# A graph layer on one core: where in a step VectorE makes its first one-hots, and which engine reads the placed sums first

## The chip, the core and the metric

The kernel runs on one core of a Trainium2 chip. The core has five engines with instruction queues of their own: TensorE (PE: matmuls, with PEld for its weight loads), VectorE (DVE), ScalarE (ACT), GpSimd (POOL) and SyncE (SP, which here only starts transfers). They meet through semaphores. The metric is the time of one execution on the device in microseconds (us); lower is better. Before the change the median of three runs is 1567.36 us (1563.31 to 1572.13).

## The reference

A message-passing layer over a graph of 6250 nodes with 64 features and 200000 edges, sorted by destination, with a residual and a layer norm around it:

```
w    = silu(edge_attr @ W1 + b1) @ W2 + b2                # 32 -> 64 -> 9 per edge
msg  = einsum('ef,em,fmg->eg', x[src], edge_sh * w, W_tp) # 64 x 9 x 64
agg  = segment_sum(msg, dst) / sqrt(16)
gamma, beta = split(silu(c_noise[:,None] @ Wn1 + bn1) @ Wn2 + bn2)
out  = layernorm(x + agg * (1 + gamma) + beta)
```

Everything is float32.

## The kernel before

**Tiling.** The edges are cut into tiles of 128, and 16 tiles make a block; there are 98 blocks and 49 groups of 128 nodes. The main loop runs over i = 0 to 97. Its order is written out by hand: what a step calls first stands first in each engine's queue. In one step different blocks are at different stages.

**Rows of the sources.** The tile `hs` of a block holds the 64 features of each edge's source. Most of its 16 tiles are fetched by indirect DMAs, one per tile, which GpSimd issues for block i+6 at the head of step i (`gather`, line 91). The last 3 or 4 tiles of a block (`picked`) are not fetched: `pick` (lines 463 to 486) selects them with matmuls. VectorE makes a one-hot `hot_k` (`hots`, line 460, 128 x 896) from the edge's key, which ScalarE has spread into PSUM (`keys`, line 454, bank tag "r"). TensorE multiplies it with the table `xs`, split in two parts, in 14 matmuls into `px` (line 475, two banks), and VectorE selects and sums the result into `hs` (lines 484 and 486). In every sixth block one more tile is fetched row by row by SyncE (line 106).

**Weights and messages.** For block i+2, `hidden` computes the first layer (line 403, bank tag "p1") and ScalarE the silu (`st`, line 411). For block i+1, `second` (line 420, bank tag "s") computes the second layer, and `weights` turns it and builds `a`, which holds the nine weights times a one-hot of the destination (lines 430, 436, 442). `windows(i)` multiplies `hs` with `a` (line 504), ScalarE copies the result into `zt` (line 514), and in odd steps `project` applies W_tp to two blocks (line 543, the bank of tag "p1" again) and turns the result (line 549); `halves` splits it in two parts `r` and makes one-hots `c` of the nodes (lines 524 to 528).

**Nodes.** `nodes(i)` takes the one bank of tag "s", called `ps`, and returns small parts that `pick` runs one by one behind its matmul pairs:
- `product`, the gate's matmul for node group i-2 (line 589), as long as i-2 is below 49;
- in even steps `place`: two matmuls (line 559) add the projected rows into the node columns `pd`. VectorE adds the carry of the pair before to the left half (`yt`, line 565), and ScalarE copies the right half as the new `carry` (line 568);
- in every fourth step (i = 7, 11, ..., 95) `bring`: two matmuls (line 576) turn two node groups back, and `finish_nodes` (lines 669 to 683) does gate, residual and layer norm on VectorE, with the square root on ScalarE. I call these finish steps;
- `gate`: VectorE reads the product into `gam` and `xb` (lines 355 and 356), in steps 2 to 50.

After these reads the "s" bank is free, and `second(i+1)` takes it for line 420 in the same step.

**Order in a step.** gathers and loads; `keys(i+2)` and the first two one-hots of block i+2; `pick(i+1, 0)` with the parts of `nodes(i)` inside it; the other one-hots; `hidden(i+2)`; `second(i+1)`; `windows(i)`; `project`; `pick(i+1, 1)` with the parts of `weights` and the turning inside it; the remaining picks.

Of the kernel before, what the change touches and what calls it, by code (L numbers as in the profile page):

```python
# [7 lines left out]
F32 = mybir.dt.float32  # L8
# [7 lines left out]
P = 128  # L16
N, F, M, D, H, E = 6250, 64, 9, 32, 64, 200000
NJ = 49
# [26 lines left out]
def pair(q):  # L45

    return [g for g in (2 * q - 1, 2 * q) if 0 <= g < NBLK]


def picked(g):  # L50

    return Q - (3 * g % 8 < 3)


def tiles(g):
    return min(KB, NT - g * KB)
# [3 lines left out]
def gnn_resnorm_kernel(ctx: ExitStack, tc: tile.TileContext, x, src, dst, dst_row, ea, sh, cn,  # L60
                       w1, b1, w2, b2, wtp, wn1, bn1, wn2, bn2, out):
    nc = tc.nc
# [16 lines left out]
    with ExitStack() as fast:  # L79
        loads = fast.enter_context(tc.tile_pool(name="loads", bufs=3))  # L80
        work = fast.enter_context(tc.tile_pool(name="work", bufs=2))
# [16 lines left out]
        def load_rows(g, e0):  # L98
            for e in range(e0, min(e0 + SPR, P), 8):
                n = min(8, min(e0 + SPR, P) - e)  # L100
                _, vs = nc.values_load_multi_w_load_instructions(
                    src_r[SPG.index(g):SPG.index(g) + 1, e:e + n], engines=[mybir.EngineType.SP],
                    min_val=0, max_val=NPAD - 1,
                    skip_runtime_bounds_check_because="src is below N, as for the gathers")
                for k in range(n):
                    nc.sync.dma_start(hs[g][e + k:e + k + 1, 0, :], x[bass.ds(vs[k], 1), :])
# [246 lines left out]
        def gate(j, pe):  # L353

            nc.vector.tensor_scalar(gam[:, j, :], pe[:, 0:F], 1.0, 0.25, op0=ALU.add, op1=ALU.mult)
            nc.vector.tensor_add(xb[:, j, :], xb[:, j, :], pe[:, F:2 * F])  # L356
# [94 lines left out]
        def keys(g):  # L451

            pk_t[g] = psum.tile([P, Q, P], F32, tag="r", name=f"pk{g}")
            nc.scalar.copy(pk_t[g][:, 0:picked(g), :], kr_t.pop(g))  # L454

        def hots(g, t0, t1):

            for t in range(t0, min(t1, picked(g))):
                hot_k[g, t] = late.tile([P, J, P], F32R, tag="hot_k", name=f"hot_k{g}_{t}", bufs=7)
                nc.vector.tensor_tensor(hot_k[g, t], pk_t[g][:, t, None, :].to_broadcast([P, J, P]),  # L460
                                        nk.unsqueeze(2).to_broadcast([P, J, P]), op=ALU.is_equal)

        def pick(g, t, other=()):


            other = [f for fs in other for f in fs]
            q = picked(g) if g < NBLK else 0
            if t >= q:
                for f in other:
                    f()  # L470
                return
            px = psum.tile([P, F, J], F32, tag="px", name=f"px{g}_{t}", bufs=2)
            for h in range(J):
                for i in range(2):
                    nc.tensor.matmul(px.rearrange("p f l -> p (f l)"), hot_k[g, t][:, h, :],  # L475
                                     xs[i][:, h].rearrange("p f l -> p (f l)"),
                                     start=(h == 0 and i == 0), stop=(h == J - 1 and i == 1))
                    if i == 1 and other:
                        other.pop(0)()
            for f in other:  # L480
                f()
            xm = late.tile([P, F, J], F32, tag="xm", name=f"xm{g}_{t}")
            c = (g + 1) * Q - q + t
            nc.vector.scalar_tensor_tensor(xm, li[:, None, :].to_broadcast([P, F, J]), jl[:, c:c + 1], px,  # L484
                                           op0=ALU.is_equal, op1=ALU.mult)
            nc.vector.tensor_reduce(hs[g][:, tiles(g) - q + t, :], xm, AX.X, ALU.add)  # L486
# [31 lines left out]
        r, hot, carry, yt = {}, {}, {}, {}  # L518
# [35 lines left out]
        def place(q, pd):  # L554

            gs = pair(q)

            def part(k):
                nc.tensor.matmul(pd, r[q][:, k].rearrange("p s f -> p (s f)"), hot.pop(gs[k]),
                                 start=(k == 0), stop=(k == len(gs) - 1))  # L560
                if k == len(gs) - 1:
                    r.pop(q)
                    if q > 0:
                        yt[q - 1] = work.tile([P, P], F32, tag="yt", name=f"yt{q}", bufs=3)
                        nc.vector.tensor_add(yt[q - 1], pd[:, 0:P], carry.pop(q - 1))  # L565
                    if q < NJ:
                        carry[q] = work.tile([P, P], F32, tag="carry", name=f"carry{q}")
                        nc.scalar.copy(carry[q], pd[:, P:2 * P])  # L568

            return [lambda k=k: part(k) for k in range(len(gs))]  # L570

        def bring(j0, j1, py):


            def part(j):
                nc.tensor.matmul(py[:, j - j0], yt.pop(j), ident2, start=True, stop=True)
                if j == j1 - 1:
                    finish(j0, j1, py[:, 0:j1 - j0])

            return [lambda j=j: part(j) for j in range(j0, j1)]  # L580

        def nodes(i):


            ps = psum.tile([P, 4, P], F32, tag="s", name=f"ps{i}")
            parts = []
            if 0 <= i - 2 < NJ:
                def product(j=i - 2):
                    nc.tensor.matmul(ps[:, 2], ht[j // 4 % 2][:, j % 4], wn2a, start=True, stop=True)
                parts.append(product)  # L590
            if i % 2 == 0 and i >= 2:
                parts += place(i // 2 - 1, ps[:, 0:2].rearrange("p a n -> p (a n)"))
            j = (i - 5) // 2
            if i % 2 == 1 and i >= 5 and j % FB == FB - 1:
                parts += bring(j + 1 - FB, j + 1, ps[:, 3].rearrange("p (j f) -> p j f", f=F))
            if 0 <= i - 2 < NJ:
                parts.append(lambda: gate(i - 2, ps[:, 2]))
            return parts

        with tc.manual_schedule(), tc.tile_pool(name="temp", bufs=1) as temp:  # L600
            setup(temp)

            for i in range(NBLK):
                if i + AHEAD < NBLK:
                    gather(i + AHEAD)
                if i % LB == 0 and i + LB < NBLK:
                    if i > 0:
                        load(i + LB)
                    near(i + LB)
                if i % LB == 1 and i + 1 + LB < NBLK:  # L610
                    load_keys(i + 1 + LB)
                if i % 4 == 3 and i + 1 < NJ:
                    gate_load(i + 1)
                for g in SPG:
                    if 0 < g - i <= AHEAD:
                        load_rows(g, (AHEAD - g + i) * SPR)
                if i + 2 < NBLK:
                    keys(i + 2)
                    hots(i + 2, 0, 2)
                pick(i + 1, 0, [nodes(i)])  # L620
                if i + 2 < NBLK:
                    hots(i + 2, 2, Q)
                if 3 <= i <= 5:
                    reach(i - 3)
                if i + 2 < NBLK:
                    hidden(i + 2)
                if i + 1 < NBLK:
                    second(i + 1)
                if i < NBLK - 2:
                    windows(i)  # L630
                turn = project(i // 2) if i % 2 == 1 else []
                if i % 4 == 1 and i - 1 < NJ:
                    gate_hidden(i - 1)
                if i + 1 < NBLK:
                    pick(i + 1, 1, [weights(i + 1), turn])
                for t in range(2, Q):
                    pick(i + 1, t)
                if i == NBLK - 1:
                    for f in turn:
                        f()  # L640
                    ps = psum.tile([P, 4, P], F32, tag="s", name="ps_l")
                    for f in place(i // 2, ps[:, 0:2].rearrange("p a n -> p (a n)")):
                        f()
                    py = psum.tile([P, FB, F], F32, tag="r", name="py_l")
                    for f in bring(NJ - 3, NJ - 1, py):
                        f()
                if i >= NBLK - 2:
                    windows(i)
                if i == NBLK - 2:
                    sums(i + 1)  # L650
            project(NBLK // 2)
            ps = psum.tile([P, 4, P], F32, tag="s", name="ps_n")
            for f in place(NBLK // 2, ps[:, 0:2].rearrange("p a n -> p (a n)")):
                f()
            for f in bring(NJ - 1, NJ, psum.tile([P, 1, F], F32, tag="r", name="py_n")):
                f()
# [201 lines left out]
```

## Time and profile before

The profiled execution took 1570.09 us; its span from first to last instruction is 1568.3 us. The granted TensorE clock was 0.972 of full speed on average.

| engine | busy us | share | instructions |
|---|---|---|---|
| PE | 1460.5 | 93% | 10810 |
| PEld | 1208.6 | 77% | 10810 |
| DVE | 1139.5 | 73% | 1987 |
| ACT | 528.6 | 34% | 1335 |
| POOL | 1129.5 | 72% | 1201 |

| group | count | mean ns | busy us |
|---|---|---|---|
| L475 px matmuls | 4970 | 375 | 1100.8 |
| L91 gathers | 1192 | 946 | 1128.2 |
| L460 hot_k | 355 | 1081 | 370.5 |
| L484 xm | 355 | 677 | 240.4 |
| L486 sum into hs | 355 | 620 | 220.1 |
| L442 a | 98 | 1353 | 132.6 |
| L411 st | 98 | 1114 | 109.2 |
| L568 carry | 48 | 265 | 12.7 |

Matmuls overlap and their ends are modelled, so a busy PE row is not PE at its peak. In a row of the groups, the first number after the bar is the busy time, the second the mean of one, and behind the second bar stands the engine's idle time just before such instructions with what ended it. In a row of waits the numbers are the total, the count and the longest. A timeline row has start, length, engine, line, operation, result <- operands, how many are merged, and in brackets the idle time before it with what ended it.

### The profile page before, as it was taken

To read this page: it belongs to the slowest core of one execution; us is meant where nothing else is said; L and a number is where in the kernel's file an instruction comes from. 1 tells how busy PE (TensorE), PEld (TensorE's weight loads), DVE (VectorE), ACT (ScalarE), POOL (GpSimd) and SP (SyncE) were. 2 spreads that over 40 slices of the span, in tenths; PEclk is the share of its full clock that TensorE was granted. 3 is DMA by queue.
4 is the path that set the end of the run, shared out by engine and by line. 5 is a ranking of instruction groups with operands and counts; after the bars stand their busy time and mean duration, and the time that the engine had idled before them with its cause. 6 is when DMAs were issued, how large, how long until landed. Compare 5 with 4: busy or idle time off the path is not lost.

```text
span 1568.3 us, 34363 instructions
## 1 busy us (share of the span) xinstructions
PE 1460.5 (93%) x10810; PEld 1208.6 (77%) x10810; DVE 1139.5 (73%) x1987; ACT 528.6 (34%) x1335; POOL 1129.5 (72%) x1201
## 2 busy tenths in 40 slices
PE   4998999999999999999999999999999999999995
PEld 2787778778787788787877877877877878778774
DVE  5686777777777777777777777777777677777773
ACT  4232242433332423332333323323233332333331
POOL 7777777777777777777777777777777777777700
PEclk9999999999999999999999999999999999999997
DMA  5321222222222222222222222222222222222200
GB/s 166 93 62 55 53 75 51 63 56 71 57 62 65 63 54 61 56 71 59 58 71 53 59 53 71 59 53 70 53 60 55 68 54 58 71 53 59 71 7 5
DMA packets 90939, 96.16 MB, mean 61 GB/s; under 512 B 37161, under 2 KB 51451, under 8 KB 90748
## 3 DMA queue, kind: packets, MB, share of 16 engines
q1 hardware_dynamic: 51842, 53.09, 11.5%
q0 software_dynamic: 38144, 39.14, 11.4%
q8 instruction: 88, 1.44, 0.4%
q10 hardware_dynamic: 762, 1.64, 0.3%
q14 instruction: 103, 0.84, 0.2%
HBM read 92.04 MB, written 1.73 MB: 60 GB/s over the span
## 4 chain that ended last, share of the span: by engine, by line
PE 51%; POOL 20%; DVE 13%; issue 8%; DMA 4%; ACT 3%; SPq 0%; DVEq 0%; POOLq 0%; ACTq 0%
PE px L475 37%; POOL hs L91 20%; DVE hot_k L460 5%; PE pz L504 5%; DMA hs<-in_x_dram,src_i 4%; PE pt L543 3%; PE p L420 2%; DVE xm L484 2%; DVE hs L486 2%; PE p L403 1%; PE p L430 1%; ACT L411 1%; ACT st L411 1%; DVE oh L382 1%; ACT carry L568 1%
## 5 line engine op out<-in xcount | busy, mean ns | idle before, releaser
L91 POOL DMA_INDIRECT hs<-in_x_dram,src_i x1192 | 1128.2, 946 | 364.0 <-issue 335.0
L475 PE MATMUL px<-xs,hot_k 128*128 128x448 f32 x4970 | 1100.8, 375 | 8.4 <-DVE xs L294 7.8
L475 PEld LDWEIGHTS px<-xs,hot_k 128*128 128x128 f32 x4970 | 903.3, 190 | 96.7 <-issue 12.2
L484 DVE SCALAR_TENSOR_TENSOR xm<-li,jl,px 128x448 f32<-128x448 f32 x355 | 240.4, 677 | 220.2 <-PE px L475 217.9
L460 DVE TENSOR_TENSOR hot_k<-pk,nk 128x896 fp32r<-128x896 f32 x355 | 370.5, 1081 | 2.3 <-ACT pk L454 2.3
L486 DVE TENSOR_REDUCE hs<-xm 128x64 f32<-128x448 f32 x355 | 220.1, 620 | 12.5 <-DVE xm L484 0.2
L514 ACT COPY zt<-pz 64x160 f32<-64x160 f32 (+2 forms) x784 | 213.3, 272 | 23.0 <-PE pz L504 13.9
L411 ACT ACTIVATE st<-p,b1c 128x1024 f32<-128x1024 f32 x98 | 109.2, 1114 | 296.1 <-PE p L403 295.8
L568 ACT COPY carry<-ps 128x128 f32<-128x128 f32 x48 | 12.7, 265 | 390.2 <-DVE yt L565 382.4
L436 DVE TENSOR_TENSOR p<-p,sh 128x72 f32<-128x72 f32 x196 | 47.3, 241 | 132.7 <-ACT rt L546 47.7
L504 PEld LDWEIGHTS pz<-a,hs 128*64 128x64 f32 x3126 | 110.6, 142 | 41.9 <-issue 38.4
L442 DVE TENSOR_TENSOR a<-oh,p 128x1152 f32<-128x1152 f32 x98 | 132.6, 1353 | 3.3
L504 PE MATMUL pz<-a,hs 128*64 128x72 f32 x3126 | 125.5, 236 | 1.1 <-DMA hs<-in_x_dram,src_i 0.6
L403 PE MATMUL p<-ea,w1bd 64*128 64x512 f32 x392 | 113.5, 656 | 0.0
L420 PEld LDWEIGHTS p<-st,w2p 128*32 128x32 f32 x784 | 16.6, 108 | 113.3 <-issue 52.7
L543 PE MATMUL pt<-zt,wtc 128*64 128x128 f32 x960 | 72.8, 305 | 27.7 <-ACT st L411 26.0
L420 PE MATMUL p<-st,w2p 128*32 128x256 f32 x784 | 63.7, 395 | 35.7 <-DVE xb L356 32.0
L543 PEld LDWEIGHTS pt<-zt,wtc 128*64 128x64 f32 x960 | 62.2, 157 | 29.7 <-ACT st L411 27.8
L679 ACT ACTIVATE var<-var,eps 128x2 f32<-128x2 f32 (+1 forms) x25 | 7.4, 296 | 220.5 <-DVE var L678 220.5
L430 PE MATMUL p<-ident,p2s 128*128 128x128 f32 x196 | 54.4, 278 | 0.0
L454 ACT CAST pk<-kr 128x384 f32<-128x384 f16 (+1 forms) x98 | 53.9, 550 | 1.5 <-DMA kr<-kd 1.4
L403 PEld LDWEIGHTS p<-ea,w1bd 64*128 64x128 f32 x392 | 30.2, 188 | 28.8 <-issue 27.9
(122 smaller groups left out, 530.0 us busy)
## 6 DMA issues: line engine op xcount, KB each, us to landing
hs<-in_x_dram SPq DMA_DIRECT2D x2048, 0.2 KB
ea<-in_ea_dram SPq DMA_DIRECT2D x49, 512.0 KB
hs<-in_x_dram,src_i POOLq DMA_INDIRECT x1192
kr<-kd SPq DMA_DIRECT2D x49, 256.0 KB
sh<-in_sh_dram SPq DMA_DIRECT2D x49, 144.0 KB
cb<-cn_d SPq DMA_DIRECT2D x12, 128.0 KB
out_dram<-o SPq DMA_DIRECT2D x24, 64.0 KB
gam<-in_x_dram ACTq DMA_DIRECT2D x2, 448.0 KB
```

Source lines behind the costliest of these rows:

```text
L91: hs_dma[g] = [nc.gpsimd.indirect_dma_start(out=hs[g][:, t - g * KB, :], out_offset=None, in_=x, in_offset=bass.IndirectOffsetOnAxis(ap=sr ...
L403: nc.tensor.matmul(p1[:, i, :], w1bd[i * 64:(i + 1) * 64, :], e[i * 64:(i + 1) * 64, :], start=True, stop=True)
L411: nc.scalar.activation(st[g], p1_t.pop(g), AF.Silu, bias=b1c)
L420: nc.tensor.matmul(p2[g][c * D:(c + 1) * D, 0, :].rearrange("p (i e) -> p i e", i=2), w2p, s[:, :, c * P:(c + 1) * P], start=True, stop=True)
L442: nc.vector.tensor_mul(a[g], oh_t.pop(g)[:, :, None, :].to_broadcast([P, KB, M, W]), sw.unsqueeze(3).to_broadcast([P, KB, M, W]))
L460: nc.vector.tensor_tensor(hot_k[g, t], pk_t[g][:, t, None, :].to_broadcast([P, J, P]), nk.unsqueeze(2).to_broadcast([P, J, P]), op=ALU.is_ ...
L475: nc.tensor.matmul(px.rearrange("p f l -> p (f l)"), hot_k[g, t][:, h, :], xs[i][:, h].rearrange("p f l -> p (f l)"), start=(h == 0 and i ...
L484: nc.vector.scalar_tensor_tensor(xm, li[:, None, :].to_broadcast([P, F, J]), jl[:, c:c + 1], px, op0=ALU.is_equal, op1=ALU.mult)
L486: nc.vector.tensor_reduce(hs[g][:, tiles(g) - q + t, :], xm, AX.X, ALU.add)
L504: mm = nc.tensor.matmul(pz[v * F:(v + 1) * F, k // 2].rearrange("p m w -> p (m w)"), hsg[:, k0 + k, :], ag[:, k0 + k].rearrange("p m w -> ...
L514: nc.scalar.copy(z[h * F:(h + 1) * F, 0:5 - h, k0 + v:k0 + n:2, :].rearrange("p m k w -> p k m w"), pz[v * F:(v + 1) * F, 0:(n + 1 - v) // ...
L543: nc.tensor.matmul(pt[h * F:(h + 1) * F, 0, 0:P], wtc2[:, c, :], z[h][:, c], start=(c == 0), stop=(c == 4))
```

## The change

Two edits. The first two one-hots of block i+2 are no longer issued ahead of `pick(i+1, 0)`. They become the last of the parts that `pick` runs behind its matmul pairs, after those of `nodes(i)`. In VectorE's queue they thus stand behind `yt` or the finish chain and behind the gate's two reads, and still ahead of `xm` of that pick. `keys(i+2)` stays where it was. And in `place` ScalarE's copy of the carry is issued ahead of VectorE's sum, so that the sum waits for the copy where the copy waited for the sum.

```
                 if k == len(gs) - 1:
                     r.pop(q)
+                    if q < NJ:
+                        carry[q] = work.tile([P, P], F32, tag="carry", name=f"carry{q}")
+                        nc.scalar.copy(carry[q], pd[:, P:2 * P])
                     if q > 0:
                         yt[q - 1] = work.tile([P, P], F32, tag="yt", name=f"yt{q}", bufs=3)
                         nc.vector.tensor_add(yt[q - 1], pd[:, 0:P], carry.pop(q - 1))
-                    if q < NJ:
-                        carry[q] = work.tile([P, P], F32, tag="carry", name=f"carry{q}")
-                        nc.scalar.copy(carry[q], pd[:, P:2 * P])
...
+                more = []
                 if i + 2 < NBLK:
                     keys(i + 2)
-                    hots(i + 2, 0, 2)
-                pick(i + 1, 0, [nodes(i)])
+                    more = [lambda: hots(i + 2, 0, 2)]
+                pick(i + 1, 0, [nodes(i), more])
```

## The prediction

> **What bounds the kernel now.** I read the page first. TensorE is busy 93%, VectorE 73%, and GpSimd 72%. GpSimd's figure misleads. The group of its gathers, on the page, and the instructions of line 91 say:
>
> ```profile
> L91 POOL DMA_INDIRECT hs<-in_x_dram,src_i x1192 | 1128.2, 946 | 364.0 <-issue 335.0
> ...
> L91 POOL DMA_INDIRECT hs<-in_x_dram,src_i x1192: 940/944/1302, 2.9 to 1493.2; - x199
> ```
>
> From 2.9 to 1494.2 us the queue never rests: each gather of 0.946 us is followed by about 0.3 us of issue, 1.25 us together, and it waits for nothing longer. So GpSimd is a clock that runs by itself, and it stops 74 us before the end only because it gathers 6 blocks ahead.
>
> How far ahead is it? I counted line 91's instructions in order (a block has 16 rows less 3 or 4 picked ones, less one more in every sixth block) against line 504's. Block 50's last gather ends at 781.7 and TensorE uses it at 837.2; block 94's ends at 1455.4 and is used at 1502.1. Apart from the first thirty blocks the lead is 45 to 56 us. So today TensorE is the slower of the two, by those 50 us. The chain of waits puts 20% on line 91; with such a lead I take this for a later gather's signal on a shared semaphore, not for a wait.
>
> Next the waits of TensorE, whose two large rows are:
>
> ```profile
> PE p L420 <- DVE xb L356: 32.0, 34, 2.2
> PE pt L543 <- ACT st L411: 26.0, 12, 2.2
> ```
>
> The timeline shows both in a finish step (i mod 4 = 3, every fourth). First i=47, with the gate; then i=71, after the gate has ended:
>
> ```profile
> 786.18 2.08 DVE L460 TENSOR_TENSOR hot_k<-pk,nk 128x896 fp32r<-128x896 f32 x2
> 786.40 0.33 PE L576 MATMUL ps<-ident,yt 128*128 128x64 f32 x2
> 788.18 0.28 DVE L669 TENSOR_TENSOR y<-ps,gam 128x128 f32<-128x128 f32 x1
> 791.19 0.21 DVE L356 TENSOR_TENSOR xb<-xb,ps 128x64 f32<-128x64 f32 x1
> 791.55 0.64 PE L420 MATMUL p<-st,w2p 128*32 128x256 f32 x8 [2.10 <-DVE xb L356]
> ```
>
> ```profile
> 1148.62 2.08 DVE L460 TENSOR_TENSOR hot_k<-pk,nk 128x896 fp32r<-128x896 f32 x2
> 1150.62 0.28 DVE L669 TENSOR_TENSOR y<-ps,gam 128x128 f32<-128x128 f32 x1
> 1152.76 0.30 ACT L679 ACTIVATE var<-var,eps 128x2 f32<-128x2 f32 x1 [10.65 <-DVE var L678]
> 1153.07 1.28 ACT L411 ACT_TABLE_LOAD   x1
> 1154.37 1.11 ACT L411 ACTIVATE st<-p,b1c 128x1024 f32<-128x1024 f32 x1
> 1155.54 2.40 PE L543 MATMUL pt<-zt,wtc 128*64 128x128 f32 x20 [2.16 <-ACT st L411]
> ```
>
> In both VectorE makes two one-hots first, and the reads of the bank stand behind them: y starts 1.4 to 2 us after its matmul. At 47 the bank is freed late for line 420. At 71 y frees it in time, but the square root, ScalarE's table load and st come late, and line 543 needs st's bank.
>
> An even step, i=46:
>
> ```profile
> 773.14 0.28 DVE L565 TENSOR_TENSOR yt<-ps,carry 128x128 f32<-128x128 f32 x1
> 773.46 0.27 ACT L568 COPY carry<-ps 128x128 f32<-128x128 f32 x1 [6.86 <-DVE yt L565]
> 773.90 0.21 DVE L356 TENSOR_TENSOR xb<-xb,ps 128x64 f32<-128x64 f32 x1
> 774.25 0.64 PE L420 MATMUL p<-st,w2p 128*32 128x256 f32 x8 [0.38 <-DVE xb L356]
> ```
>
> VectorE, ScalarE, VectorE take turns on the bank, and line 420 is 0.45 us later than where it follows line 403 without a wait (there it starts 0.07 us before 403's modelled end).
>
> Last, the clock, in stretches of 3.41 us (behind start, end and length stand the busy times of the five engines; the third number from the right is the granted clock):
>
> ```profile
> 1090.59:1094.00 3.41, 1.45 (x21) 1.28 (x22) 3.21 (x5) 3.35 (x8) 2.50 (x4) 1.00 0.61 158
> 1094.00:1097.41 3.41, 3.41 (x11) 2.85 (x11) 1.32 (x3) 1.24 (x5) 2.59 (x3) 0.50 0.35 111
> ```
>
> TensorE idles in the first (the wait of line 543 at i=67) and runs the next at half clock. Steady state has 14 such stretches, 8 before and 6 after i=51, all in finish steps behind the 2 us wait. They cost about 1.6 us each: step 67 takes 20.11 us, step 59, as long in work but undisturbed, 18.47.
>
> [...]
>
> **The change part by part.** No instruction is added or removed; GpSimd's and SyncE's order stays. T is the start of px_0, the step's first pick. VectorE has finished the step before at T+1.54 us.
>
> *One-hots behind the reads, finish steps with gate (i=7 to 47, 11 of them).* The last bring matmul ends at 786.73, so y starts at 786.77 instead of 788.18, 1.41 us earlier, and the chain to xb, which holds ScalarE's square root, moves with it. Line 420 then starts at 790.14; without a wait it would be 789.38. st ends at 791.63, line 543 is due at 791.7, so no second wait takes over. 11 x 1.41 = 15.5 us.
>
> *Finish steps without gate (51 to 95, 12).* Bring ends at 1148.53, VectorE is free at 1148.62: y 2.00 us earlier. st ends at 1153.48, line 543 starts at 1153.54, against 1153.2 without a wait. 12 x 2.0 = 24 us.
>
> *Even steps.* Placing ends at 771.19; carry to 771.5, yt, gam, xb to about 772.4, while line 403 ends at 773.87. The wait goes: 24 steps (4 to 50) x 0.45 = 10.8 us. Later even steps lose 0.15+0.07 us to the carry: 22 x 0.22 = 4.8 us. The swap's own cost is ScalarE's 0.27 us before yt, hidden under those 1.5 us; without that cover it would be about 0.3 us a step, 15 us in all. ScalarE arrives early: it sat idle 6.86 us before its copy.
>
> *What becomes later.* Behind the waiting yt or y stand the two one-hots (2.08 us) and then xm_0. Their readers come a step later. In the finish step xm_0 starts at T+7.3 instead of T+6.6 (gate) or T+6.5 instead of 6.3. px_2 wants xm_0's bank at about T+11.4: 3.5 us of room, 4 in even steps. Then VectorE's row: one-hots to T+10.6, line 436 to 11.1 (11.5 today), `a` to 12.5, r and c to 13.1, xm_1 to 13.8, before the next step's px_0 needs that bank at T+14.2. In a finish step of three picks VectorE ends 1.55 us into the next step, as now. Tight, but it holds. Steps i mod 4 = 1 gain nothing.
>
> *Sum of the waits*: 15.5+24+10.8+4.8 = 55 us. *Clock*: the idle stretch falls from 2.1 to 0.3-0.8 us, so the 14 slow stretches should go: 22 us. TensorE alone would end 55 to 77 us earlier.
>
> *Where it goes.* That is more than the lead. By i=50, 39 us are gained of 55.6; by i=64 to 67 the lead (47) is used up, or with the clock term absent, only at the end. From there TensorE waits for gathers at line 504. I take each block's last gather, its 2.4 us to landing (the chain's rows) and today's time from that block's line 504 to the last block's, less what is still gained behind it. The last block's own: 1494.2+2.4 = 1496.6. Block 94's: 1455.4+2.4+48.5 less 3.9 = 1502.4, and block 95's 1472.8+33.3 less 3.8 = 1502.3. With no gain in the clock 1504; TensorE's own row then says 1550.5-55 = 1495. So both ways the last windows start near 1502.4, not at 1550.5: 48 us. The tail behind, 17.8 us, stays: span 1520. The profiled run took 1570.1, 1.8 over its span and 2.7 over the median of 1567.4; so I forecast 1520 as the median, 47 us or 3.0% less.
>
> **Rivals.**
> - *GpSimd caps the gain* (forecast, 1520; 1511 to 1528): chance 0.65. Its end cannot move: last landing plus tail is a span of 1514.4, some 1513.5 as a median, a floor whatever else improves.
> - *Half of the finish gain*, because VectorE reaches y later than I reckon, or a second wait is left at line 543: 20+15.6 = 35 us, no clock gain, TensorE bound to the end: 1532, up to 1545. For: the finish steps leave VectorE no slack. 0.22.
> - *It doesn't do what it says*: the waits of 420 and 543 go, and the same time returns at px_1 or line 430. For: 420 and 543 lie in series. Against: in steps i mod 4 = 1 the same row runs without a wait. About 1562; 0.05.
> - *Slower*: the one-hots ahead of xm_0 hold the bank that px_2 needs. It needs VectorE 3.5 us later than worked out; beyond that each microsecond costs 96 us, and at 0.57 us a step the 55 are eaten. At 1 us a step: 1567+96-55 = 1608. Against: today VectorE waits 218 us in all for px, never px for xm. 0.05.
>
> The remaining 0.03 is a small gain. SyncE's row copies I leave out: they come 15 to 29 us ahead of use, and SyncE still waits 47 us for line 504 and 110 us for VectorE.
>
> **Numbers.** Three runs of before lie within 0.6%, so 0.5% is about what can be told from no change. Range 1511 (the floor less 0.2%) to 1540 (most of the half-gain case). Faster 0.90, within 0.5% 0.05, slower 0.05.
>
> **What would show it.** y right behind its matmul; no wait of 420 for xb over 0.8 us; st's wait at 543 under 0.5 us; fewer half-clock stretches before i=60; gathers still ending near 1494; the lead at block 94 down from 47 to a few us and line 504 waiting for hs in the last third. Wrong if VectorE's px waits vanish and px waits for xm, or if the lead stays above 20 us.

## The result, and the profile after

The changed kernel takes 1520.83 us (median of four runs, 1520.56 to 1521.78), against 1569.74 us for the kernel before in the runs beside it (1563.31 to 1577.18). The ratio is 0.9688, with a 95% interval of 0.9642 to 0.9733: 3.1% faster, where 3.0% and 1520 us were forecast. The profiled execution took 1521.78 us, with a span of 1519.9 us and a granted clock of 0.983.

**The finish steps.** First the timeline of the same two steps as before, i=47 with the gate and i=71 without it:

```profile
748.96 0.33 PE L576 MATMUL ps<-ident,yt 128*128 128x64 f32 x2
749.33 0.29 DVE L670 TENSOR_TENSOR y<-ps,gam 128x128 f32<-128x128 f32 x1 [0.50 <-PE ps L576]
752.42 0.21 DVE L356 TENSOR_TENSOR xb<-xb,ps 128x64 f32<-128x64 f32 x1
752.54 2.08 DVE L460 TENSOR_TENSOR hot_k<-pk,nk 128x896 fp32r<-128x896 f32 x2
752.77 0.64 PE L420 MATMUL p<-st,w2p 128*32 128x256 f32 x8 [0.77 <-DVE xb L356]
```

```profile
1103.40 0.28 DVE L670 TENSOR_TENSOR y<-ps,gam 128x128 f32<-128x128 f32 x1
1105.54 0.29 ACT L680 ACTIVATE var<-var,eps 128x2 f32<-128x2 f32 x1 [9.90 <-DVE var L679]
1106.28 2.08 DVE L460 TENSOR_TENSOR hot_k<-pk,nk 128x896 fp32r<-128x896 f32 x2
1107.15 1.12 ACT L411 ACTIVATE st<-p,b1c 128x1024 f32<-128x1024 f32 x1
1108.32 1.31 PE L543 MATMUL pt<-zt,wtc 128*64 128x128 f32 x20 [0.15 <-ACT st L411]
```

The one-hots now stand below the finish chain's reads. In step 47 y starts 0.04 us after its matmul ends (748.96+0.33), where it started 1.45 us after; line 420 waits 0.77 us instead of 2.10. In step 71 line 543 waits 0.15 us for st instead of 2.16.

**An even step**, i=46:

```profile
733.92 0.28 PE L559 MATMUL ps<-c,r 128*128 128x256 f32 x1
734.24 0.27 ACT L565 COPY carry<-ps 128x128 f32<-128x128 f32 x1 [4.63 <-PE ps L559]
734.54 0.29 DVE L568 TENSOR_TENSOR yt<-ps,carry 128x128 f32<-128x128 f32 x1 [0.30 <-ACT carry L565]
734.88 0.21 DVE L356 TENSOR_TENSOR xb<-xb,ps 128x64 f32<-128x64 f32 x1
735.01 2.08 DVE L460 TENSOR_TENSOR hot_k<-pk,nk 128x896 fp32r<-128x896 f32 x2
736.81 0.64 PE L420 MATMUL p<-st,w2p 128*32 128x256 f32 x8
```

The copy now waits for the placing and the sum for the copy. The bank is free at 735.1, 1.7 us before line 420, which waits for nothing.

**Where TensorE waits now**, from its waits (total, count, longest):

```profile
PE pz L504 <- DMA hs<-in_x_dram,src_i: 11.5, 8, 4.4
PE pz L504 <- issue: 10.8, 6, 4.8
...
PE p L420 <- DVE xb L356: 7.8, 11, 0.8
...
PE pt L543 <- ACT st L411: 1.0, 6, 0.2
```

The two large rows of before, 32.0 and 26.0 us, are down to 7.8 and 1.0, and line 504 waits 22 us in its two rows. The same view's "issue" row at line 504 is put down to nothing in the profile; at i=83 it is 4.82 us long and ends at 1291.11, while the block's last gather instruction ended at 1287.86 and the chain of waits leads to a gather landing at 1289.44. I count it with the gathers. The profile puts one more wait of line 504, 2.5 us at i=91, down to the landing of a store; what held it is not shown.

**The gathers and the last windows**, first line 91's instructions, then TensorE's timeline:

```profile
L91 POOL DMA_INDIRECT hs<-in_x_dram,src_i x1192: 940/944/1300, 2.9 to 1493.2; - x199
```

```profile
1456.99 1.22 PE L504 MATMUL pz<-a,hs 128*64 128x72 f32 x32
1472.36 1.22 PE L504 MATMUL pz<-a,hs 128*64 128x72 f32 x32 [0.41 <-DMA hs<-in_x_dram,src_i]
...
1502.01 1.67 PE L504 MATMUL pz<-a,hs 128*64 128x72 f32 x22
```

GpSimd starts its last gather at 1493.2, to the tenth as before. Counted in order as before, the gathers of blocks 94 and 95 end at 1455.45 and 1470.45, so TensorE uses them 1.5 and 1.9 us later, where the lead had been 47 us. The last block's windows start at 1502.0 instead of 1550.5.

**The clock**, over 862 us of steady state (the third number from the right):

```profile
137.88:1000.00 862.12, 849.48 (x6525) 709.04 (x6523) 675.05 (x1192) 309.85 (x792) 651.94 (x690) 1.00 0.26 62
```

The granted clock is 1.00 there, with no stretch at half clock, where before had eight (0.98 by the same view). Four come later (at 1090, 1169, 1292 and 1411, 3.41 us each), each in a step in which line 504 waits 2.3 to 4.8 us. The prediction had not reckoned with them.

### The profile page after: what moved, and what is told of

The parts are those of the page before. It is cut to its first block, busy times and chain, and to the rows that moved or that the text cites. A ratio compares the mean times of both kernels' runs of the same rounds, so it can differ in the third digit from the quotient of the medians.

```text
span 1519.9 us, 34363 instructions
## 1 busy us (share of the span) xinstructions
PE 1438.0 (95%) x10810; PEld 1192.7 (78%) x10810; DVE 1135.4 (75%) x1987; ACT 526.1 (35%) x1335; POOL 1129.3 (74%) x1201
## 3 DMA queue, kind: packets, MB, share of 16 engines
q10 hardware_dynamic: 762, 1.64, 0.3%
## 4 chain that ended last, share of the span: by engine, by line
PE 57%; POOL 18%; issue 9%; SPq 5%; DMA 5%; DVE 4%; ACT 2%; DVEq 0%; POOLq 0%; ACTq 0%
PE px L475 41%; POOL hs L91 18%; PE pz L504 5%; DMA hs<-in_x_dram,src_i 4%; PE p L403 3%; SPq L106 3%; PE pt L543 3%; PE p L420 2%; SPq L101 2%; PE p L430 1%; PE ps L559 1%; PE ps L589 0%; ACT st L411 0%; DVE hot_k L460 0%; DVE xm L484 0%
## 5 line engine op out<-in xcount | busy, mean ns | idle before, releaser
L543 PE MATMUL pt<-zt,wtc 128*64 128x128 f32 x960 | 64.3, 281 | 2.6 <-ACT zt L514 1.7
L543 PEld LDWEIGHTS pt<-zt,wtc 128*64 128x64 f32 x960 | 55.0, 142 | 3.8 <-ACT zt L514 1.9
```

What stands on the lines that cost most here:

```text
L543: nc.tensor.matmul(pt[h * F:(h + 1) * F, 0, 0:P], wtc2[:, c, :], z[h][:, c], start=(c == 0), stop=(c == 4))
```

## The experiments

The theory: two waits of TensorE and the half-clock stretches behind them fall away, worth about 77 us, and the gathers let only 48 of them through. The rivals: the waits were worth just 47 us and there is no cap; the swap of copy and sum carries part of the gain; VectorE's one-hots, now later, cost something.

"Light" kernels take the cap away. They leave out part of the computation: the gather of tile 2 of each block isn't made, and line 504 multiplies tile 1's rows in its place. TensorE's instructions stay the same in number and size.

```
-                for t in range(g * KB + (g in SPG), g * KB + tiles(g) - picked(g))]
+                for t in range(g * KB + (g in SPG), g * KB + tiles(g) - picked(g)) if t - g * KB != 2]
...
-                                          hsg[:, k0 + k, :], ag[:, k0 + k]...
+                                          hsg[:, k0 + k - (k0 + k == 2), :], ag[:, k0 + k]...
```

### A first set on a chip where it could not be answered

The first four kernels ran on a chip on which the kernel before takes 2574 us. With these kernels it is 57 to 66% slower than the chips used for the other runs, so only ratios to its own runs of before count.

> Only the first edit: the two one-hots behind the reads; carry and sum in the old order. Theory (GpSimd caps the gain): finish steps gain as in the changed kernel, and even steps too, since the reads come before line 403 ends in either order; TensorE alone would gain more than the cap lets through, so 1520 (1518 to 1525), equal to both edits together. Rival (no cap, the two edits add up and the swap brings the 15.6 us of the even steps): about 1536.

> Only the second edit: the carry ahead of the sum, one-hots in front as before. Theory: the finish steps keep their 2 us waits and their half-clock stretches; in even steps gam need not wait for the carry, which loses 24 x 0.3 to 0.45 and 22 x 0.22 us, 12 to 15 us: about 1553, gathers not yet a limit. Rival (VectorE comes to the sum late anyway, so the order of sum and copy is without effect): 1567.

> The changed kernel with one gather less in each block: the rows of tile 2 are not fetched, the rows of tile 1 are multiplied in their place, all other work the same. It leaves out 98 of 1192 gathers, so GpSimd would end near 1371 us. Theory (GpSimd caps, TensorE alone gains 55 us of waits and 22 us of clock): 1490 to 1497. Without the clock term: about 1513. Rival (no cap; the waits removed were just worth 47 us): 1520, as the changed kernel.

> The kernel before with the same gather of each block left out (tile 1's rows used for tile 2). Theory (before the change TensorE was the limit and gathers led by 50 us): no change, 1562 to 1570. Rival (gathers already slow the kernel before, by waits or by competing for DMA and memory): faster by 1% or more.

Measured: 2524 us (0.978, 0.969 to 0.988), 2571 us (0.999, 0.997 to 1.001), 2422 us (0.941, 0.932 to 0.950) and 2455 us (0.955, 0.946 to 0.963). The waits of the first one:

```profile
POOL hs L91 <- PE pz L504: 929.3, 89, 29.8
DVE xm L484 <- remote: 642.0, 106, 58.1
...
PE px L475 <- DVE xm L484: 512.7, 68, 12.4
```

GpSimd waits 929 us for TensorE and line 504 waits under 1 us in all, so no gather limits TensorE, and VectorE waits 642 us for signals whose sender the profile doesn't show. The forecast's numbers don't apply to such a kernel. Two things can be kept: the one-hots gain here too, about 2%, and the swap alone does not. That TensorE waits for xm on this chip is not the edit's doing: in the light kernel without either edit it waits 451 us for it as well. Why leaving out a gather that TensorE doesn't wait for saves 4.5% here, I don't know.

### The cap taken away, on a chip like that of the result

The kernel before takes 1564.5 us here (1560.0 to 1575.6).

> The changed kernel with one gather less in each block (the rows of tile 2 are not fetched, tile 1's rows are multiplied in their place, all other work the same), so 98 of 1192 gathers are left out and GpSimd would end near 1371 us where the kernel before takes 1567. Theory (gathers cap the gain; TensorE alone gains 55 us of waits and 22 us of clock): 0.950 to 0.955 of the kernel before, 1490 to 1497. Without the clock term 0.965, 1513. Rival (no cap; the waits were just worth 47 us): 0.969, 1520, as the changed kernel.

Measured: 1489.61 us (1488.62 to 1490.52), ratio 0.9522 (0.9471 to 0.9573). Its instructions of line 91, its instructions of line 504 and its waits of TensorE:

```profile
L91 POOL DMA_INDIRECT hs<-in_x_dram,src_i x1094: 938/944/1300, 2.9 to 1375.3; - x183
```

```profile
L504 PE MATMUL pz<-a,hs x3126: 225/226/383, 54.4 to 1470.0; 128*64 128x72 f32 x196
```

```profile
PE p L420 <- DVE xb L356: 7.8, 11, 0.8
...
PE pt L543 <- ACT st L411: 1.8, 11, 0.2
```

The gathers end over 90 us before the last windows, line 504 waits for them about 1 us in all, and 31 us more are gained over the changed kernel. So TensorE was held back by the gathers, and the rival without a cap falls.

> The kernel before with the same gather of each block left out. Theory (before the change the gathers led by 50 us and limited nothing): 0.996 to 1.002 of the kernel before. Rival (gathers cost the kernel before time by waits or by competing for DMA and memory): below 0.99.

Measured: 1567.29 us, ratio 1.0014 (0.9994 to 1.0034). Its waits of TensorE are those of the kernel before:

```profile
PE p L420 <- DVE xb L356: 31.6, 33, 2.2
PE pt L543 <- ACT st L411: 25.9, 12, 2.2
```

Before the change the gathers cost nothing that can be told from noise. The two light kernels differ by 78 us, which is the whole worth of the change with the cap gone; 77 were worked out.

### Each edit alone

> Only the second edit, the carry ahead of the sum; one-hots in front as before. Theory: finish steps keep their 2 us waits and half-clock stretches; in even steps gam no longer waits for the carry, 24 x 0.3 to 0.45 and 22 x 0.22 us: 12 to 15 us, 0.990 to 0.993, about 1554. Rival (VectorE comes to the sum late anyway, the order is without effect): 0.998 to 1.002.

Measured: 1544.57 us (1544.18 to 1546.02), ratio 0.9870 (0.9817 to 0.9923); 20 us, more than forecast. Waits of TensorE, and the even step i=46 in the timeline:

```profile
PE pt L543 <- ACT st L411: 26.1, 12, 2.3
PE p L420 <- DVE xb L356: 23.2, 11, 2.2
```

```profile
754.01 2.08 DVE L460 TENSOR_TENSOR hot_k<-pk,nk 128x896 fp32r<-128x896 f32 x2
754.10 0.27 ACT L565 COPY carry<-ps 128x128 f32<-128x128 f32 x1 [4.63 <-PE ps L559]
756.01 0.28 DVE L568 TENSOR_TENSOR yt<-ps,carry 128x128 f32<-128x128 f32 x1
756.34 0.21 DVE L356 TENSOR_TENSOR xb<-xb,ps 128x64 f32<-128x64 f32 x1
756.70 0.64 PE L420 MATMUL p<-st,w2p 128*32 128x256 f32 x8
```

The copy is made while VectorE makes its one-hots, so sum and gate run on without a pause and line 420 doesn't wait, although the one-hots still come first. The eleven and twelve waits of the finish steps are all there. Step by step (from one step's first pick to the next's), this profile and that of the kernel before differ in two places. The even steps are 15.9 us shorter in all, near the 12 to 15 forecast. The finish steps are 7.5 us shorter: steps that are at half clock in only one of the profiles differ by 1.5 to 1.7 us each, the others by no more than 0.3. The clock's records show 9 half-clock stretches in the steady state of this profile, against 14 before (granted clock 0.978 and 0.972 over the whole run). So the swap itself is worth some 16 us, and the rest is the smaller number of stretches. That number differs between profiles with the same waits: the kernel before with a gather left out has 16. What decides it is not shown; the last section sets two such waits side by side.

> Only the first edit, with the gather of tile 2 left out as in the light kernels. Theory: the one-hots alone remove the waits of finish steps and even steps (the reads come before line 403 ends in either order of copy and sum), so within 2 us of the changed kernel with the same gather left out, 1490 to 1499. Rival (the even steps need the swap): 10 to 16 us above it.

Measured: 1488.01 us (1487.47 to 1488.66), 1.6 us below both edits with the same gathers left out. The swap adds nothing to the first edit.

> Only the first edit, all gathers made. Theory (with the gather of tile 2 left out it was as fast as both edits, so TensorE alone is at 1488; the gathers cap the rest): 0.967 to 0.972 of the kernel before, 1519 to 1523, the same as both edits. Rival (the swap is needed for the last part of the gain): 1526 or more.

Measured: 1521.58 us (1520.86 to 1521.95), before 1567.80; ratio 0.9695 (0.9647 to 0.9743). All of the gain is had without the swap, and TensorE waits at line 504 as in the changed kernel:

```profile
PE pz L504 <- DMA hs<-in_x_dram,src_i: 12.2, 10, 4.1
...
PE pz L504 <- issue: 11.9, 7, 4.9
```

### The finish steps alone

```
-                    hots(i + 2, 0, 2)
-                pick(i + 1, 0, [nodes(i)])
+                    if i % 4 != 3:
+                        hots(i + 2, 0, 2)
+                more = [lambda: hots(i + 2, 0, 2)] if i % 4 == 3 and i + 2 < NBLK else []
+                pick(i + 1, 0, [nodes(i), more])
```

This is on the kernel before, with the light kernels' gather left out.

> One-hots behind the reads in finish steps alone (i mod 4 = 3), old order elsewhere, no swap, the gather of tile 2 left out. Theory: keeps the even steps' waits, 24 x 0.45 and 22 x 0.22 = 15.6 us above 1488: 1502 to 1505, no half-clock stretch in the steady state. If the finish steps' waits and stretches were worth less than 39.5 and 22 us: above 1510.

Measured: 1508.31 us (1507.65 to 1509.38), 20.3 us above the light kernel with all one-hots moved, where 15.6 were expected. Its waits of TensorE:

```profile
PE p L420 <- DVE xb L356: 16.6, 33, 0.9
...
PE pt L543 <- ACT st L411: 1.9, 11, 0.3
```

No half-clock stretch is left in the steady state (granted clock 0.989 over the whole run). So by these medians the finish steps, waits and clock together, are worth 1567.3-1508.3 = 59 us (61.5 worked out), and the even steps 20. Step by step against the other light kernel, the 24 even steps up to 50 are 0.55 us longer each and the 22 later ones 0.30, not 0.45 and 0.22. The rest is not at line 420: in some even steps, before the change as well, the later picks run longer (step 56 takes 15.12 us, step 54 with the same work 14.89). The cause of that stays open. Set step by step against the profile of the kernel before, with its 14 stretches, the light kernel with all one-hots moved has finish steps 61.8 us shorter and even steps 17.5 us shorter.

### A version that beats both

If GpSimd is the cap at 1520.8 and TensorE could do 1488, work can be moved from one to the other: 8 more tiles are picked by matmul instead of gathered. The result is the same.

```
-    return Q - (3 * g % 8 < 3)
+    return Q - (3 * g % 8 < 3 and g % 16 != 3 and g not in (38, 70))
```

> The changed kernel with 8 more tiles picked by matmul and so 8 gathers less (363 picks, 1184 gathers), the result the same. Theory (gathers cap at 1520.8, TensorE alone at 1488): the cap falls by 8 x 1.25 = 10 us, TensorE's row grows by 8 x 2.8 = 22 us, they meet: 1509 to 1514, 0.964 to 0.967 of before, 0.5% faster than the changed kernel. Rival (TensorE's picks are not covered): 1520 plus 22, 1543.

Measured: 1511.34 us (1510.78 to 1512.06, six runs), ratio 0.9631 (0.9595 to 0.9667): 9.5 us less than the changed kernel. The intervals of the two ratios overlap, since the runs of before vary, but its slowest run lies 8.5 us below the changed kernel's fastest. On its own chip, the first edit with all gathers took 1521.58 us, 10.2 us more. Its gathers:

```profile
L91 POOL DMA_INDIRECT hs<-in_x_dram,src_i x1184: 940/945/1294, 2.9 to 1482.2; - x198
```

They end 11 us earlier, and line 504 waits 2.3 us for them in all, where it waited 22. At block 62 the gathers still lead by 18.8 us, and the lead is down to 1.5 us only at block 94. With 8 more picks the two limits all but meet.

## Why the prediction was right, point by point

The total alone is weak evidence for the terms behind it: by the prediction's own sums the cap gives nearly the same end with the clock term or without it. The light kernels are what tests the terms.

- *GpSimd as a clock of its own*: right. Its last gather starts at 1493.2 in both profiles, and taking the gathers' cap away moves the changed kernel (1489.6) and not the one before (1567.3).
- *Finish steps with gate, 1.41 us each*: right. Line 420's wait was forecast at 0.76 us and is 0.69 to 0.77. *Without gate, 2.0 us each*: right, 0.15 us left of 2.16. With the clock 59 us were measured for 61.5 by the medians, 61.8 in the profiles.
- *Even steps, 15.6 us*: right in kind, somewhat too small. Measured are 15.9 us with the swap alone, 17.5 from the kernel before to the light kernel with the one-hots moved, and 20 above that light kernel when only the finish steps are changed. The term per step was read from line 420 alone. And I gave these steps to both edits; either one is enough, for different reasons: with the one-hots moved, the turns on the bank end before line 403 does (705.89 and 707.55 in an even step of the light kernel with the first edit alone); with the swap, sum and gate follow each other without ScalarE's copy in between, from 756.01 to 756.55 in the even step shown.
- *The clock, 22 us*: right for the 14 stretches of that profile. Steady state has none of them in both light kernels with the one-hots moved (granted clock 0.989 over the whole run), and the finish steps became 61.8 us shorter where 39.5+22 were worked out. The 14 is in part luck: the same waits gave 9 and 16 in other profiles.
- *What becomes later*: right. On the chip of the result VectorE still waits for px (202 us) and TensorE never for xm after the setup, so 3.5 us of room was enough.
- *The lead and where it is used up*: forecast at i = 64 to 67. At i=50 15.0 us were left of 55.6. It first fell to 1.6 us at i=62, and the first wait of more than 1 us at line 504 stands at i=64, with 3.0 us.
- *The end*: the last windows were forecast at 1502.4 and start at 1502.0. Two of the terms were off, and part of the error cancels. The landing was misread: the 2.4 us of the chain run from the start of a gather, as the chain and the timeline of the kernel before show, and I added them to its end.

```profile
589.41 2.38 DMA hs<-in_x_dram,src_i
```

```profile
589.41 0.94 POOL L91 DMA_INDIRECT hs<-in_x_dram,src_i  x1 [0.30 <-issue]
```

That leaves 1.4 us behind the end, and blocks 94 and 95 were used 1.5 and 1.9 us behind it. So the floor of the forecast was about 1 us too high. The row from block 94 to the end took 45.0 us, not 44.6.

- *The rivals*: half of the finish gain, the same time at a later wait, and the slower case by xm's bank are refuted by the light kernels. The swap's cost, 0.27 us under other work, was rightly nothing, but its worth beside the first edit is nothing either.

## What to carry to other kernels

VectorE ran its instructions in the order of issue: at i=47 y started 1.45 us after its matmul, behind two one-hots whose readers come a step later. In such a queue put what frees a shared bank ahead of work that is needed later, and price the move at the engine that waits, not at the one that is moved. Before adding up the waits that fall, look for an engine whose queue never rests but which works ahead: here its lead of 47 us was about all that could be gained (48 us in the profiles), and its last item plus the tail gave a floor that could be read from the profile of before. When such a cap is reached, the next gain lies in shifting work off that engine, here 8 gathers for 8 picks.

## What the runs showed of the hardware that was not expected

- Waits of TensorE of nearly the same length were followed by half clock or not. Between the setup and the last blocks the clock's records show 14 half-clock stretches in the profile of before and four in that of the changed kernel. Each is 3.41 us long, and in the 3.41 us ahead of each TensorE idled 1.85 us or more. But 1.88 us of idle time in the 3.41 us from 1284.76 of the changed kernel were followed by full clock, so these numbers give no sure limit. The same 23 waits of 2.1 to 2.3 us gave 14, 16 and 9 stretches in three profiles. At i=83 of the kernel before, a wait of 2.21 us ends at 1337.99. The stretch in which it ends and the one behind it (busy time of TensorE behind the length):

```profile
1336.35:1339.76 3.41, 1.77 (x23) 1.53 (x24) 2.89 (x4) 3.34 (x9) 2.50 (x4) 1.00 0.71 196
1339.76:1343.17 3.41, 3.41 (x20) 3.11 (x19) 2.48 (x6) 1.58 (x6) 2.50 (x4) 1.00 0.24 69
```

The clock stays full after 1.64 us of idle time, where 1.96 us in the stretch at 1090.59, with a wait of 2.21 us at i=67, were followed by half clock. What decides between two such waits is not shown.

- A gather's landing took longer at one place. At i=83 of the changed kernel it is 3.78 us in the chain of waits instead of 2.4, with loads of 512 and 144 KB and a store just issued and 163 GB/s moving, against 45 GB/s in another stretch. TensorE then waited 4.82 us. That the other transfers are the cause is not shown.
- After the square root ScalarE's table load of 1.28 us is all that the silu pays: the root ends at 1153.06 in the profile of before, the silu starts at 1154.37.
- One chip ran the kernel before in 2574 us, at a granted clock near 0.81, where others took 1565 to 1570 us at about 0.97. In the kernel with the first edit, the gathers and the one-hots took as long there as in the kernel before elsewhere (947 and 1081 ns, against 946 and 1081), so the time is not in GpSimd's and VectorE's own instructions. The first edit gained 2.2% there and 3% on another chip. What makes that chip slower stays open.
